# Mamba scan kernel: the sums over the states of two slots issued together, and a skip addition moved by one slot

## Chip, cores and metric

The kernel runs on one core of a Trainium2 chip, in one launch. The metric is the device time of the launch in microseconds (us); lower is better.

## What is computed

The reference applies two layers to x, of shape (4, 512, 64, 64), in float32. The first is a group norm, then a Mamba block run on four groups of 128 channels, then a projection; the second is a group norm and a linear attention. Both add their input. This case concerns the recurrence inside the Mamba block and what follows it:

```python
def step(h, inp):
    dt_t, B_t, C_t, x_t = inp
    dA = jnp.exp(dt_t[:, :, None] * A)
    h = dA * h + (dt_t * x_t)[:, :, None] * B_t[:, None, :]
    y = jnp.einsum('bds,bs->bd', h, C_t)          # sum over the 16 states
    return (h, y)
...
y = ys.transpose(1, 0, 2) + xc * D_param
y = y * jax.nn.silu(z)
return jnp.einsum('bld,od->blo', y, out_proj_w)
...
ym = ym + skip_scale * chunks                     # the skip addition
```

There are 256 inner channels, 16 states, and 4096 positions for each of 4 images and 4 channel groups.

## The kernel before, in words

The outer loop has 128 steps: image b (4), time tile t of 512 positions (8), channel group c (4). A step has 16 slots. A slot s covers one half e of the 256 inner channels, one quarter q of the states (4 of 16), and, by `jj`, two of the four blocks of 32 channels: partition 32k+i of a tile holds state k of the four and channel i of a block. So slots s = 0 to 7 are e = 0 and 8 to 15 are e = 1, and an even slot has blocks 0 and 1, the odd one after it blocks 2 and 3, with the same states. The global slot number is g.

What a slot does, in the order in which `slot` (from L457) emits it:

- `keep(g - 1)` (L494), on POOL: a copy of the last column of h, 128x2.
- `b_row` (L428), on SP, in odd slots: the rows of B for a later pair of slots, broadcast by four DMAs from DRAM.
- `drive(g + 1)` (L453), on POOL: the product of `d_all` and `b_all`, 128x1024, into a buffer `bx` for the next slot. There are three `bx` buffers, so it writes the one that slot g - 2 used.
- two scans (L470), on DVE, 128x512 each, reading `bx` and `dA`, writing h; after each a `decay` (L445) on ACT, the exponential for a later scan, into one of two PSUM banks.
- the multiply (L478), on DVE: h times `c_all`, written back into the same `bx`.
- in odd slots `c_row` (L84, named `c_all`), on PE: the rows of C for the next pair of slots, spread over the partitions into the only `c_all` bank.
- the sums over the states, here called the fold (L84, named `y<-bx,fold`), on PE: for each of the slot's two blocks a matmul of `bx` with a 128x32 matrix of ones and zeros, which adds four states and writes 32 partitions of the bank `y`. Four quarters accumulate there. `bx` is free when both are done.
- `after()`: everything else, spread over the slots by a fixed list and by three queues of pieces.

`after()` and `in_scan()` put this into the slots: `with_d` (L499, reads `y`) in slots 0 and 8; `gate` (L502, POOL) in 1 and 9; `time_banks` (`pt`, PE) in 1; the softplus (ACT) and `out_proj` (`po`, two PE matmuls for the step before) in 2; `with_skip` (L511, DVE, reads `po`) and `to_rows` (L370, a POOL product, and two DMAs) in 3; the pieces of `inputs` (`pc`, `pz`) in 3 to 7; silu in 10; `mixers` (`pd`) from 11. After these, one piece at most of the queue `late` (norms of the next time tile, projection of the last one) and one of `rest` (attention of the image before) is emitted, as long as a credit in matmul units lasts. All orders on all engines are fixed when the program is built (`manual_schedule`); an engine's instructions run in that order.

In float32 each matmul instruction appears in the trace as two weight loads and two passes.

Of the kernel before, what the change touches and what calls it, by code (L numbers as in the profile page):

```python
# [24 lines left out]
def kernel(  # L25
# [26 lines left out]
    NC = C // P  # L52
# [6 lines left out]
    BLK = 32  # L59
    KS = P // BLK  # L60
    NQ = NST // KS
    NJ = P // BLK
# [12 lines left out]
    def work_bank(name):  # L75
        return ps_w.tile([P, T], F32, tag="w", name=name)
# [4 lines left out]
    def mm(out_, lhsT, rhs, **how):  # L81

        work["mm"] += (0.25 if rhs.dtype == BF16 else 1.0) * rhs.shape[-1] / T
        nc.tensor.matmul(out_, lhsT, rhs, **how)  # L84

    work = {"mm": 0.0}
# [27 lines left out]
    for i in range(3):  # L114
        r = slice(i * LANE, (i + 1) * LANE)
# [6 lines left out]
    fold = const.tile([P, BLK], F32, tag="fold", name="fold")  # L122
    for k in range(KS):
        r = slice(k * BLK, (k + 1) * BLK)
# [83 lines left out]
    for o in range(NC):  # L208
        pw = work_bank(f"pw_{o}")
        for c in range(NC):  # L210
            mm(
                pw[:, 0:1], w_pr[:, c, o * P : (o + 1) * P], b_sb[:, c : c + 1],
                start=(c == 0), stop=(c == NC - 1),
# [45 lines left out]
    def bc(v, n):  # L259
        return v.unsqueeze(1).to_broadcast([P, n, v.shape[-1]])  # L260
# [152 lines left out]
    JJ = NJ // 2  # L413
    SLOTS = NH * NQ * JJ

    def place(g):

        n, r = divmod(g, SLOTS)
        e, r = divmod(r, NQ * JJ)
        return n, e, *divmod(r, JJ)  # L420

    b_all, c_all, dAs, bxs, hs, ys = {}, {}, {}, {}, {}, {}

    def b_row(g):
        n, e, q, _ = place(g)
        got = wk.tile([P, T], F32, tag="b_all", name=f"b_all_{g}", bufs=3)
        for k in range(KS):
            nc.sync.dma_start(  # L428
                got[k * BLK : (k + 1) * BLK, :],
                fs[n]["b_rows"][q * KS + k, :].partition_broadcast(BLK),  # L430
            )
        b_all[g // JJ] = got
# [16 lines left out]
    def drive(g):  # L449
# [5 lines left out]
        )  # L455

    def slot(g, last, in_scan, after):  # L457
        n, e, q, jj = place(g)
        b, t, c = steps[n]
        js = slice(jj * 2, jj * 2 + 2)  # L460
        if g:
            keep(g - 1)
        if g % JJ and g + 5 < last:
            b_row(g + 5)
        if g + 1 < last:
            drive(g + 1)
        h = hs[g] = wk.tile([P, 2, T], F32, tag="h", name=f"h_{g}", bufs=2)
        for i in range(2):
            j = jj * 2 + i
            nc.vector.tensor_tensor_scan(  # L470
                h[:, i, :], dAs.pop(2 * g + i), bxs[g][:, i, :],
                0.0 if t == 0 else st[b][:, c, e, q, j : j + 1], ALU.mult, ALU.add,
            )
            if 2 * g + i + LEAD < 2 * last:
                decay(2 * g + i + LEAD)
        in_scan()

        nc.vector.tensor_tensor(bxs[g], h, bc(c_all[g // JJ], 2), ALU.mult)  # L478
        if g % JJ and g + 1 < last:
            c_row(g + 1)  # L480
        if q == 0 and jj == 0:
            ys[n, e] = ps_y.tile([P, T], F32, tag="y", name=f"y_{n}_{e}")
        for i in range(2):
            r = slice((jj * 2 + i) * BLK, (jj * 2 + i + 1) * BLK)
            mm(ys[n, e][r, :], fold, bxs[g][:, i, :], start=(q == 0), stop=(q == NQ - 1))
        work["mm"] -= 1
        del bxs[g]
        after()

    def keep(g):  # L490

        n, e, q, jj = place(g)
        b, _, c = steps[n]
        nc.gpsimd.tensor_copy(st[b][:, c, e, q, jj * 2 : jj * 2 + 2], hs.pop(g)[:, :, T - 1])  # L494
# [9 lines left out]
    def out_proj(f, nm):  # L504
        f["po"] = work_bank(f"po_{nm}")
        for e in range(NH):
            mm(f["po"], w_op[:, e, :], f["xz"][:, 1, e, :], start=(e == 0), stop=(e == NH - 1))

    def with_skip(f, xn, c):
        v = xn[:, c, NTAP - 1 : NTAP - 1 + T]  # L510
        nc.vector.scalar_tensor_tensor(v, v, sk, f["po"], ALU.mult, ALU.add)  # L511
# [129 lines left out]
    steps = [(b, t, c) for b in range(B) for t in range(NT) for c in range(NC)]  # L641
# [3 lines left out]
    xn, pads = {}, {}  # L645
# [19 lines left out]
    def leave(b, t):  # L665
        if t == 0:
            stats1[b] = stats_tile(f"st1_{b}")
            x1s[b] = [
                dram.tile([P, NC, T], F32, tag="x1", name=f"x1_{b}_{i}", bufs=3 * NT)
                for i in range(NT)  # L670
            ]
        ym = xn[b, t][:, :, NTAP - 1 : NTAP - 1 + T]
        yield from projected(ym, stats1[b], x1s[b][t], b, t)
        if t == NT - 1:
            yield
            norms[b, 1] = stats_end(stats1[b], f"b{b}")
            rest.append(attention(b, x1s[b], norms[b, 1]))
            yield
# [8 lines left out]
    late, rest, light = [], [], []  # L687
# [30 lines left out]
    with tc.manual_schedule():  # L718
        credit = 0.0
        for n, (b, t, c) in enumerate(steps):  # L720
            f, nm = fs[n], names[n]
            before = fs[n - 1] if n else None
            nxt = fs[n + 1] if n + 1 < N else None
            front = step_inputs(n + 2) if n + 2 < N else iter(())
            mix = mixers(fs[n + 2], names[n + 2]) if n + 2 < N else iter(())
            if c == 0 and (t + 1 < NT or b + 1 < B):
                late.append(tile_norm(b, t + 1) if t + 1 < NT else tile_norm(b + 1, 0))
            if c == 0 and t == 0 and b + 1 < B:
                light.append(input_norm(b + 1))
                st[b + 1] = wk.tile([P, NC, NH, NQ, NJ], F32, tag="st", name=f"st_{b + 1}")  # L730
            if c == 2:
                while late and (b, t + 1) in xn and late[0].__name__ == "tile_norm":
                    one(late)
            for s in range(SLOTS):
                def in_scan():
                    if s == 0 and before is not None:
                        with_d(before, n - 1, 1)
                    if s == SLOTS // 2:
                        with_d(f, n, 0)

                def after():
                    nonlocal credit
                    start = work["mm"]
                    if s == 1:
                        spread(f, 1, nm)
                        if before is not None:
                            gate(before, 1)
                        if nxt is not None:
                            time_banks(nxt, names[n + 1])
                    if s == 2:  # L750
                        if nxt is not None:
                            nc.scalar.preload_act_table_set("softplus")
                            time_steps(nxt, names[n + 1])
                            nc.scalar.preload_act_table_set("natural_log_exp_and_others")
                        if before is not None:
                            out_proj(before, names[n - 1])
                    if s == 3:
                        if before is not None:
                            pb_, pt_, pc_ = steps[n - 1]
                            with_skip(before, xn[pb_, pt_], pc_)  # L760
                            if pc_ == NC - 1:
                                late.append(leave(pb_, pt_))
                        if nxt is not None:
                            to_rows(nxt, 0, names[n + 1])
                            to_rows(nxt, 1, names[n + 1])
                    if 3 <= s < 8:
                        next(front, None)
                    if s == 10 and n + 2 < N:
                        silu(n + 2)
                        nc.scalar.preload_act_table_set("natural_log_exp_and_others")  # L770
                    if s == 9:
                        gate(f, 0)
                        if nxt is not None:
                            spread(nxt, 0, names[n + 1])
                    if s >= 11:
                        next(mix, None)
                    if s in (2, 10):
                        one(light)
                        credit = 0.0
                        return  # L780
                    credit = min(credit + 3.2 - (work["mm"] - start), 3.2)
                    for queue in (late, rest):
                        if credit > 0:
                            start = work["mm"]
                            one(queue)
                            credit -= work["mm"] - start

                slot(n * SLOTS + s, N * SLOTS, in_scan, after)
            fs[n - 1].clear() if n else None
        keep(N * SLOTS - 1)  # L790
# [60 lines left out]
```

## Time and profile before

| what | value |
|---|---|
| median of 3 runs | 9795.15 us (9785.57 to 9796.92) |
| the profiled execution, its own time | 9786.31 us |
| its span in the profile | 9784.6 us |
| slots (steps), from the first scan to the last multiply | 123 us to 9299 us |
| DVE busy | 8325.7 us (85%) |
| PE busy, all matmuls | 7861.1 us (80%) |
| of which the fold, 8192 records | 2566.8 us |
| POOL busy | 6088.6 us (62%) |
| ACT busy | 5018.9 us (51%) |
| mean granted TensorE clock | 0.863 |

The profile's page gives the busy time of each engine, then the span in 40 slices, then groups of instructions with their busy time, the mean duration of one, and the idle time of the engine just before them with what ended it. The trace behind it can be asked for waits (who waited for whom) and for a timeline. The stretch after 9299 us has no slots: there the attention of the last image runs, with PE busy and DVE nearly idle.

### The profile page before, as it was taken

The numbers are of one execution on the slowest core, as the hardware profiler recorded it, in microseconds if no ns is written. First come the engines' busy times: TensorE is split into PE (matmuls) and PEld (weight loads), VectorE is DVE, ScalarE is ACT, GpSimd is POOL, SyncE is SP. The second block draws the span as 40 slices with busy tenths as digits, with TensorE's granted clock in tenths as the row PEclk, the third lists the DMA queues.
The fourth block names the chain that finished last, engine by engine and source line by source line (L and its number), as shares of the span: only waits on it lengthen the run. The fifth ranks groups of instructions, "written<-read, shape, count | busy, mean of one in ns | idle before, by whom it ended". The sixth has DMA issues, their size and how long they took to land.

```text
span 9784.6 us, 75975 instructions
## 1 busy us (share of the span) xinstructions
PE 7861.1 (80%) x20192; PEld 2424.5 (25%) x20192; DVE 8325.7 (85%) x7474; ACT 5018.9 (51%) x6944; POOL 6088.6 (62%) x4949
## 2 busy tenths in 40 slices
PE   5777777777788888888888888888888888888889
PEld 1111111111222222222222222222222222222244
DVE  6998898889899999888898989988988999988910
ACT  4554555555555555545555555555555555554421
POOL 3766666666666666666666666666666666666600
PEclk8777777777888889889888989989888989988999
DMA  5455444444545445545555554445554444555512
GB/s 145 122 125 126 108 113 116 117 116 120 134 121 132 120 117 128 124 124 146 137 131 129 125 128 116 117 120 137 151 127 117 123 120 121 122 124 134 143 37 78
DMA packets 628210, 1196.87 MB, mean 122 GB/s; under 512 B 116056, under 2 KB 116576, under 8 KB 615488
## 3 DMA queue, kind: packets, MB, share of 16 engines
q1 hardware_dynamic: 620928, 1187.44, 48.6%
q10 hardware_dynamic: 6848, 4.57, 0.2%
q8 instruction: 159, 2.61, 0.1%
q14 instruction: 275, 2.25, 0.1%
HBM read 986.04 MB, written 205.52 MB: 122 GB/s over the span
## 4 chain that ended last, share of the span: by engine, by line
PE 42%; DVE 38%; issue 11%; ACT 5%; DMA 3%; POOL 1%; SPq 0%; DVEq 0%; ACTq 0%; POOLq 0%
DVE h L470 27%; PE y L84 10%; PE pc L84 9%; DVE bx L478 7%; PE pq L84 4%; PE pt L84 3%; PE pr L84 3%; PE pp L84 3%; PE po L84 2%; PE c_all L84 2%; PE pd L84 2%; PE mu_b L84 2%; PE pz L84 1%; DVE xn L286 1%; ACT dA L445 1%
## 5 line engine op out<-in xcount | busy, mean ns | idle before, releaser
L453 POOL TENSOR_TENSOR bx<-d_all,b_all 128x1024 f32<-128x1024 f32 x2048 | 4824.3, 2356 | 251.4 <-PE y L84 170.7
L445 ACT ACTIVATE dA<-d_all,a_t 128x512 f32<-128x512 f32 x4096 | 2789.8, 689 | 3377.1 <-DVE h L470 3358.3
L470 DVE TENSOR_TENSOR_SCAN h<-dA,st,bx 128x512 f32<-128x512 f32 x3584 | 4391.8, 1267 | 140.4 <-ACT dA L445 138.8
L84 PE MATMUL y<-bx,fold 128*32 128x512 f32 x8192 | 2566.8, 709 | 630.0 <-DVE bx L478 628.3
L478 DVE TENSOR_TENSOR bx<-h,c_all 128x1024 f32<-128x1024 f32 x2048 | 2499.5, 1220 | 152.6 <-PE c_all L84 36.7
L494 POOL COPY st<-h 128x2 f32<-128x2 f32 x2048 | 380.1, 186 | 2639.9 <-DVE h L470 2498.7
L84 PE MATMUL c_all<-parts,sel 96*128 96x512 bf16 x1024 | 447.9, 437 | 1141.0 <-DVE bx L478 1140.9
L84 PE MATMUL pq<-w_qk,xa 128*128 128x512 f32 x2048 | 995.5, 614 | 1.5 <-ACT xa L252 1.5
L84 PE MATMUL pc<-xn,w_cv 128*128 128x512 f32 x2048 | 954.8, 609 | 4.6 <-ACT xn L290 4.6
L84 PEld LDWEIGHTS y<-bx,fold 128*32 128x32 f32 x8192 | 321.5, 115 | 2345.8 <-issue 1399.6
L470 DVE TENSOR_TENSOR_SCAN h<-dA,bx 128x512 f32<-128x512 f32 x512 | 596.4, 1206 | 35.4 <-ACT dA L445 17.6
L84 PE MATMUL pp<-xn,w_pr 128*128 128x512 f32 x1024 | 548.2, 662 | 4.2 <-DVE xn L286 4.2
L84 PE MATMUL pr<-xb,m 128*128 128x512 f32 x1024 | 512.9, 635 | 42.0 <-DMA xb<-x 42.0
L84 PEld LDWEIGHTS <-sel 96*128 96x128 bf16 x1280 | 127.2, 99 | 1631.2 <-DVE bx L478 1273.0
L84 PEld LDWEIGHTS pc<-xn,w_cv 128*128 128x128 f32 x2048 | 369.8, 190 | 595.2 <-issue 485.0
L84 PEld LDWEIGHTS pq<-w_qk,xa 128*128 128x128 f32 x2048 | 393.7, 197 | 474.6 <-issue 459.1
L343 ACT ACTIVATE xz<-pc,cb 128x512 f32<-128x512 f32 x256 | 175.9, 687 | 430.2 <-PE pc L84 430.2
L370 POOL TENSOR_TENSOR dt<-dt,xz 128x1024 f32<-128x1024 f32 x128 | 301.4, 2355 | 149.9 <-ACT dt L363 149.8
L561 DVE TENSOR_TENSOR kq<-pk,kq 128x512 f32<-128x512 f32 x124 | 85.3, 688 | 320.6 <-PE pk L84 320.6
L84 PE MATMUL pd<-xz,w_xp 128*120 128x512 f32 x512 | 356.1, 832 | 0.0
L84 PE MATMUL pt<-dtr,w_dt 8*128 8x512 f32 x512 | 351.7, 819 | 1.5 <-ACT dtr L395 1.5
L511 DVE SCALAR_TENSOR_TENSOR xn<-xn,sk,po 128x512 f32<-128x512 f32 x128 | 95.6, 747 | 298.5 <-PE po L84 298.5
(132 smaller groups left out, 6454.6 us busy)
## 6 DMA issues: line engine op xcount, KB each, us to landing
d_all<-d_rows SPq DMA_DIRECT2D x2048, 256.0 KB, 6.9
b_all<-b_rows SPq DMA_DIRECT2D x4096, 64.0 KB, 2.2
d_rows<-dt SPq DMA_DIRECT2D x256, 512.0 KB, 3.1
xs<-in_x_dram SPq DMA_DIRECT2D x32, 1024.0 KB, 11.9
xn<-in_x_dram SPq DMA_DIRECT2D x32, 1024.0 KB, 5.3
xr<-in_x_dram SPq DMA_DIRECT2D x32, 1024.0 KB, 5.3
x<-xr SPq DMA_DIRECT2D x32, 1024.0 KB, 4.3
xa<-x SPq DMA_DIRECT2D x32, 1024.0 KB, 5.5
```

The lines of the kernel that those rows point to most:

```text
L84: nc.tensor.matmul(out_, lhsT, rhs, **how)
L286: nc.vector.tensor_tensor(v, v, bc(var, NC), ALU.mult)
L343: nc.scalar.activation(xz[:, 0, e, :], pc[e], AF.Identity, bias=cb[:, e : e + 1])
L370: nc.gpsimd.tensor_tensor(f["both"][:, 1], f["both"][:, 0], f["xz"][:, 0], ALU.mult)
L445: nc.scalar.activation(dAs[k], fs[n]["d_all", e][:, 0, j, :], AF.Exp, scale=a_t[:, e, j, q : q + 1])
L453: nc.gpsimd.tensor_tensor(bxs[g], fs[n]["d_all", e][:, 1, jj * 2 : jj * 2 + 2, :], bc(b_all[g // JJ], 2), ALU.mult)
L470: nc.vector.tensor_tensor_scan(h[:, i, :], dAs.pop(2 * g + i), bxs[g][:, i, :], 0.0 if t == 0 else st[b][:, c, e, q, j : j + 1], ALU.mult, ...
L478: nc.vector.tensor_tensor(bxs[g], h, bc(c_all[g // JJ], 2), ALU.mult)
L494: nc.gpsimd.tensor_copy(st[b][:, c, e, q, jj * 2 : jj * 2 + 2], hs.pop(g)[:, :, T - 1])
L511: nc.vector.scalar_tensor_tensor(v, v, sk, f["po"], ALU.mult, ALU.add)
L561: nc.vector.tensor_tensor(kq, pk, kq, ALU.add)
```

## The change

The fold moves out of `slot` into a function of its own, which is called in odd slots only and does the four blocks of both slots of a pair one after the other: an even slot issues no matmul for `y`. Both `bx` buffers of the pair are let go there. The bookkeeping of matmul units for the credit comes to the same sum. In the loop, `with_skip` and, at the last channel group, the start of `leave` (which appends the projection's pieces to `late`) move from slot 3 to slot 4.

```diff
         nc.vector.tensor_tensor(bxs[g], h, bc(c_all[g // JJ], 2), ALU.mult)
         if g % JJ and g + 1 < last:
             c_row(g + 1)
-        if q == 0 and jj == 0:
+        if jj == JJ - 1:
+            fold_states(g)
+        after()
+
+    def fold_states(g):
+
+        n, e, q, _ = place(g)
+        if q == 0:
             ys[n, e] = ps_y.tile([P, T], F32, tag="y", name=f"y_{n}_{e}")
-        for i in range(2):
-            r = slice((jj * 2 + i) * BLK, (jj * 2 + i + 1) * BLK)
-            mm(ys[n, e][r, :], fold, bxs[g][:, i, :], start=(q == 0), stop=(q == NQ - 1))
-        work["mm"] -= 1
-        del bxs[g]
-        after()
+        for j in range(NJ):
+            mm(
+                ys[n, e][j * BLK : (j + 1) * BLK, :], fold, bxs[g + 1 - JJ + j // 2][:, j % 2, :],
+                start=(q == 0), stop=(q == NQ - 1),
+            )
+        work["mm"] -= 2
+        for i in range(JJ):
+            del bxs[g - i]
...
+                    if s == 4 and before is not None:
+                        pb_, pt_, pc_ = steps[n - 1]
+                        with_skip(before, xn[pb_, pt_], pc_)
+                        if pc_ == NC - 1:
+                            late.append(leave(pb_, pt_))
                     if s == 3:
-                        if before is not None:
-                            pb_, pt_, pc_ = steps[n - 1]
-                            with_skip(before, xn[pb_, pt_], pc_)
-                            if pc_ == NC - 1:
-                                late.append(leave(pb_, pt_))
                         if nxt is not None:
                             to_rows(nxt, 0, names[n + 1])
                             to_rows(nxt, 1, names[n + 1])
```

## The prediction, as recorded before the changed kernel ran

> **What bounds the kernel now.** I read the busy times and the groups first. After each group stand its busy time, the mean duration of one, and the idle time just before it.
>
> ```profile
> PE 7861.1 (80%) x20192; PEld 2424.5 (25%) x20192; DVE 8325.7 (85%) x7474; ACT 5018.9 (51%) x6944; POOL 6088.6 (62%) x4949
> ...
> PEclk8777777777888889889888989989888989988999
> ...
> L453 POOL TENSOR_TENSOR bx<-d_all,b_all 128x1024 f32<-128x1024 f32 x2048 | 4824.3, 2356 | 251.4 <-PE y L84 170.7
> ...
> L470 DVE TENSOR_TENSOR_SCAN h<-dA,st,bx 128x512 f32<-128x512 f32 x3584 | 4391.8, 1267 | 140.4 <-ACT dA L445 138.8
> L84 PE MATMUL y<-bx,fold 128*32 128x512 f32 x8192 | 2566.8, 709 | 630.0 <-DVE bx L478 628.3
> L478 DVE TENSOR_TENSOR bx<-h,c_all 128x1024 f32<-128x1024 f32 x2048 | 2499.5, 1220 | 152.6 <-PE c_all L84 36.7
> ```
>
> DVE sets the pace: up to 9304 us, where the slots end, it sits idle only about 900 us. Then the waits on DVE in that stretch (us in total, times, longest):
>
> ```profile
> DVE xn L511 <- PE po L84: 298.5, 88, 6.7
> DVE h L470 <- ACT dA L445: 156.4, 145, 3.4
> DVE xr L324 <- PE pp L84: 79.9, 57, 2.4
> ...
> DVE kq L561 <- PE pk L84: 58.2, 42, 3.0
> DVE xn L270 <- PE mu_b L84: 52.3, 31, 2.0
> DVE bx L478 <- PE c_all L84: 36.7, 22, 3.7
> ```
>
> A third of the idle time is the skip addition waiting for `po` in slot 3; most of the rest also waits for PE. Then the timeline, PE first, POOL second, DVE third, at one odd slot:
>
> ```profile
> 5009.02 0.38 PE L84 MATMUL c_all<-parts,sel 96*128 96x512 bf16 x1
> 5009.33 1.05 PE L84 MATMUL y<-bx,fold 128*32 128x512 f32 x4
> 5010.31 1.13 PE L84 MATMUL pz<-xn,w_z 128*128 128x512 f32 x2
> ```
>
> ```profile
> 5006.58 2.35 POOL L453 TENSOR_TENSOR bx<-d_all,b_all 128x1024 f32<-128x1024 f32 x1
> 5010.07 0.18 POOL L494 COPY st<-h 128x2 f32<-128x2 f32 x1 [1.14 <-DVE h L470]
> 5010.48 2.36 POOL L453 TENSOR_TENSOR bx<-d_all,b_all 128x1024 f32<-128x1024 f32 x1 [0.23 <-PE y L84]
> ```
>
> ```profile
> 5002.79 1.22 DVE L478 TENSOR_TENSOR bx<-h,c_all 128x1024 f32<-128x1024 f32 x1
> 5003.93 2.45 DVE L470 TENSOR_TENSOR_SCAN h<-dA,st,bx 128x512 f32<-128x512 f32 x2
> 5006.41 1.22 DVE L478 TENSOR_TENSOR bx<-h,c_all 128x1024 f32<-128x1024 f32 x1
> ```
>
> A bare slot takes DVE 3.62 us (5006.41 - 5002.79). The fold occupies PE 0.98 us (5009.33 to 5010.31), and a drive follows a fold's start by 1.15 us.
>
> **What the Trainium skill says.** "TensorEngine Tiling (Array Packing)", section Tiling Modes: 128 rows by 32 columns gives four tiles that run independently. The trace agrees for two: a fold's four records start 0, 7, 453 and 460 ns after the first, so both tiles run each pass side by side. Four are not in it. "TensorE: Matmul & The Clock Gate", Part 3: three column tiles measured 2.38x. That speaks for four going together; no run here shows it. The same page, Part 1: PE's clock halves after a quiet window of about 3.4 us. The trace agrees: the clock is at half for 2687.6 us, in stretches that are multiples of 3.4 us, and then a fold's second pass starts 855 instead of 453 ns after the first.
>
> **The fold, on PE.** The same 8192 passes, but in 1024 groups of four tiles. If four go as two do, a group costs 0.98 + 2 x 0.007, say 1.0 us, and the 1024 groups of even slots go: about 1000 us of PE at full clock. From below the gain could be nothing (two pairs in turn, 1.96 us). I take four together. PE isn't the bound; this pays only through waits.
>
> **The fold, on POOL: a new wait.** The drive of slot o+2 (o odd) reuses the buffer of the even slot before o. Today that is free a slot earlier; then it comes free only with the group after o's multiply. Queued behind that drive on POOL are the copy L494 and the next drive; the scan of o+2 waits for it. From the end of o's multiply to that scan:
> - full clock: 0.36 (`c_all` first, least delay seen in odd slots) + 1.15 + 2.36 + 0.04 (POOL to DVE) = 3.91 us;
> - half clock: 0.59 + 2.01 + 2.36 + 0.04 = 5.00 us, with the delays of the half-clock folds.
>
> A bare pair gives 3.54 to 3.61 us. So I took from the trace, for every odd slot, the DVE work and the idle time between its multiply's end and the scan two slots on. Two choices are mine. First, half of the present idle time there stays, since PE, which causes it, loses 1 us in about 6 per pair. Second, the half-clock share: now 0.41, 0, 0.10, 0.28, 0.66, 0.22, 0.34 for slots 1, 5, 7, ... 15. It rises, as PE's idle time gathers just ahead of each group. For this there is an indication: the first 512 slots, without attention work, show 0.44 of their folds at half clock, the others 0.16. Means per window in us; the two floors are means of the greater of (work + half the idle) and 3.91 or 5.00:
>
> | slot | work + idle | floor 3.91 | floor 5.00 | share | x128, us |
> |---|---|---|---|---|---|
> | 1 | 4.17 + 0.59 | 4.63 | 5.28 | 0.55 | +29 |
> | 5 | 4.60 + 1.13 | 5.21 | 5.63 | 0.10 | -61 |
> | 7 | 5.08 + 0.24 | 5.20 | 5.63 | 0.30 | +1 |
> | 9 | 4.01 + 0.21 | 4.32 | 5.14 | 0.60 | +77 |
> | 11 | 4.38 + 1.25 | 5.04 | 5.53 | 0.70 | -32 |
> | 13 | 4.83 + 0.28 | 4.98 | 5.45 | 0.50 | +13 |
> | 15 | 4.47 + 0.27 | 4.61 | 5.20 | 0.55 | +24 |
>
> For slot 9: 0.4 x 4.32 + 0.6 x 5.14 - 4.22 = 0.60, x 128 = 77. Sum: +51.
>
> **The skip addition, slot 3 to 4.** Its own 747 ns stay in the window of slot 3 (4.31 work + 2.35 idle), so only the wait counts. But `po` is late because PE is behind, and PE runs `c_all` and the group of slot 3 behind `po`. In place of the skip, the scan of slot 5 waits until 3.9 us after `po`. `po` itself comes earlier: slot 2's fold, which stood ahead of it, is gone, 0.98 us at full and 1.9 at half clock; with almost half of slot 2's folds at half clock, 1.4 us. So in each window of slot 3 I took 1.4 off the wait, and then the greater of the window's work, 3.91, and the rest of the wait + 3.9: a mean of 5.50 instead of 6.66, x 128 = -148 us, not -298. With 0.7 us earlier it is 5.90 (-97), with 1.9 it is 5.25 (-180).
>
> **Backlog.** Slots 3 and 4 issue 6.84 us of other matmuls (16 passes of 0.428), with the group 8.2 against 8.1 us of DVE work, so slot 5 inherits lateness: 0.2 us x 128 = 25. Half-clock stretches elsewhere: I add 30 more, from 0 to 110 together. Total +55.
>
> **Costed at nothing.** `leave` one slot later: `tile_norm`'s dozen pieces stand ahead of it in `late`; without them one piece in each of 32 tiles would shift, 1 us each at most. `b_row`'s DMA on SP waits for a drive some 2 us longer, and what is queued there behind it with it; its rows are used four slots (14 us) later and land in 2.2. On POOL `to_rows` (2.36) in slot 3 now ends about when the group does; at most another 0.2 us per step, 25 us, within the backlog's range. No DMA or POOL work is added.
>
> **Sum.** -148 + 51 + 55 = -42 on 9786 for the profiled execution: 9744. The median of the runs shown (9795) is 9 above that execution: about 9750.
>
> **Rivals.**
> 1. *The new wait wins (slower).* PE goes quiet between groups and sits at half clock: shares 0.70, 0.15, 0.40, 0.75, 0.80, 0.65, 0.70, three quarters of the idle stays, `po` comes only 0.7 earlier. The same table gives +222, then -97 + 80: +205, or 10000. With half of the idle staying, it decides once more than about 0.62 of the groups outside slots 3 and 5 start at half clock (mean of the shares now 0.33, in the forecast 0.53). For it: a slower DVE makes PE quieter still. Against: at half clock the same work fills PE twice as long, which ends quiet windows.
> 2. *Relief wins.* Shares stay, a quarter of the idle remains, `po` 1.9 earlier, no backlog: -155 - 180 = -335, or 9460. For it: nearly every DVE wait names PE. Against: the quarter of the run with less PE work has the slower clock.
> 3. *Four tiles don't run together*: the groups take 0.98 (full) or 1.9 (half) more, floors 4.89 and 6.9. The table over all eight slots gives +836: 10630. Against: two do run together.
>
> **Chances.** Forecast 0.43 (own range 9660 to 9880), rival 1 0.35, rival 2 0.17, rival 3 0.05. A measurement of this kernel tells about 0.2% from no change (20 us). Faster: rival 2 and 0.7 of the forecast, 0.47; within 0.2%: 0.08; slower 0.45. The range 9440 to 10080 leaves out rival 3 (0.05), the upper quarter of rival 1 (0.09) and the lower third of rival 2 (0.06).
>
> **What would show it.** Right: `y` busy near 1100 to 1500 us with eight records per group starting within 30 ns per pass; the wait of the skip for `po` gone; new waits of DVE h (L470) on POOL bx (L453), and of POOL on PE y, some hundreds of times each, most at slots 1, 9 and 11. Wrong: few such waits (rival 2), a clock below 0.80 (rival 1), records of a group starting in two pairs (rival 3).

## The result, and the profile after

The changed kernel takes 9942.35 us (median of 4 runs, 9941.46 to 9956.8), the one before 9796.03 us (4 runs, 9785.57 to 9803.79). The ratio on record is 1.0154 (the medians alone give 1.0149), with a 95% interval of 1.0136 to 1.0171: slower by 1.5%, where 0.5% faster was forecast. The profiled execution took 9941.5 us, 155 more than that of before. From the first multiply to the last it is 153 us longer; the stretch ahead of that is 5 us longer, the one behind it 3 us shorter.

The page of the changed kernel, the lines that answer to those shown of before:

```profile
PE 7108.6 (72%) x20192; PEld 2467.3 (25%) x20192; DVE 8370.9 (84%) x7474; ACT 5014.6 (50%) x6944; POOL 6023.3 (61%) x4949
...
PEclk7677776677788888878878878878878888887899
...
L453 POOL TENSOR_TENSOR bx<-d_all,b_all 128x1024 f32<-128x1024 f32 x2048 | 4817.9, 2353 | 2786.7 <-PE y L84 2655.7
L470 DVE TENSOR_TENSOR_SCAN h<-dA,st,bx 128x512 f32<-128x512 f32 x3584 | 4395.4, 1268 | 484.3 <-POOL bx L453 396.7
...
L84 PE MATMUL y<-bx,fold 128*32 128x512 f32 x8192 | 1479.8, 803 | 1.7 <-DVE bx L478 1.7
```

The change does on PE what it says: the fold is busy for 1480 us instead of 2567, and PE as a whole for 752 us less (at the lower clock, 0.798 against 0.863, its other work takes 335 us more). But POOL's drive waits 2656 us for the fold, where it waited 171, and the scan waits for the drive. The waits on DVE, up to the end of the slots (us in total, times, longest); the first fence is one line of before, for the wait that grew:

```profile
DVE h L470 <- POOL bx L453: 18.6, 3, 15.8
```

```profile
DVE h L470 <- POOL bx L453: 484.9, 599, 16.2
DVE h L470 <- ACT dA L445: 89.2, 148, 4.5
...
DVE bx L478 <- PE c_all L84: 57.9, 50, 3.2
DVE kq L570 <- PE pk L84: 52.9, 28, 3.1
DVE xr L324 <- PE pp L84: 42.3, 43, 1.4
DVE xn L270 <- PE mu_b L84: 37.1, 30, 2.0
```

The wait of the skip addition for `po` (298.5 us) is gone, and 484.9 us of a wait that was 18.6 stand in its place. One group and what hangs on it, in the timeline of PE, of POOL and of DVE, with the clock at half for the first group and at full for the second:

```profile
5009.45 0.59 PE L84 MATMUL c_all<-parts,sel 96*128 96x512 bf16 x1 [3.45 <-DVE bx L478]
5009.97 1.94 PE L84 MATMUL y<-bx,fold 128*32 128x512 f32 x8
...
5018.09 0.38 PE L84 MATMUL c_all<-parts,sel 96*128 96x512 bf16 x1 [0.80 <-DVE bx L478]
5018.39 1.07 PE L84 MATMUL y<-bx,fold 128*32 128x512 f32 x8
5019.39 0.39 PE L84 MATMUL pq<-bqk,sel 96*128 96x512 bf16 x1
```

```profile
5011.99 2.35 POOL L453 TENSOR_TENSOR bx<-d_all,b_all 128x1024 f32<-128x1024 f32 x1 [3.66 <-PE y L84]
```

```profile
5008.18 1.22 DVE L478 TENSOR_TENSOR bx<-h,c_all 128x1024 f32<-128x1024 f32 x1
...
5012.34 1.22 DVE L478 TENSOR_TENSOR bx<-h,c_all 128x1024 f32<-128x1024 f32 x1
5014.37 2.34 DVE L470 TENSOR_TENSOR_SCAN h<-dA,bx 128x512 f32<-128x512 f32 x2 [0.81 <-POOL bx L453]
```

The multiply of the odd slot ends at 5009.40 (5008.18 + 1.22). `c_all` and eight fold records follow, two passes for each of four tiles; the drive starts at 5011.99, the scan at 5014.37: 4.97 us from multiply to scan, the 5.00 of the forecast's half-clock floor. At full clock the group of eight records occupies PE for 1.00 us (5018.39 to 5019.39), against 0.98 for four records before.

The added 153 us in the slots are 61 us of idle stretches over 0.15 us, 47 us of shorter ones, 42 us in which DVE's instructions overlap less, and 3 us by which they are longer in sum. A scan that waits for nothing starts 0.08 us before the multiply ahead of it ends (5003.93 against 5002.79 + 1.22 in the trace of before); the scan at 5014.37 starts after the drive that it waits for. So a wait costs more than the idle time that is booked for it: 599 waits of 0.08 us would be 48 us, an estimate.

By odd slot, the window of the forecast (from the multiply's end to the scan two slots on), means in us, from the two traces. "Bound" counts those of the 128 windows (127 for slot 15) in which the scan starts within 0.06 us of the drive's end; the share is that of the groups whose first record starts at half clock:

| slot | before | forecast | after | bound | half-clock share forecast, found |
|---|---|---|---|---|---|
| 1 | 4.76 | 4.99 | 5.21 | 91 | 0.55, 0.49 |
| 3 | 6.65 | 5.50 | 5.70 | 97 | 0.15, 0.16 |
| 5 | 5.73 | 5.25 | 5.51 | 58 | 0.10, 0.01 |
| 7 | 5.32 | 5.33 | 5.51 | 35 | 0.30, 0.20 |
| 9 | 4.22 | 4.81 | 4.89 | 110 | 0.60, 0.59 |
| 11 | 5.63 | 5.38 | 5.71 | 71 | 0.70, 0.77 |
| 13 | 5.11 | 5.22 | 5.36 | 76 | 0.50, 0.43 |
| 15 | 4.74 | 4.93 | 5.07 | 64 | 0.55, 0.46 |

### The profile page after: what moved, and what is told of

It is laid out like the page before. It is cut to its first block, busy times and chain, and to the rows that moved or that the text cites. A ratio compares the mean times of both kernels' runs of the same rounds, so it can differ in the third digit from the quotient of the medians.

```text
span 9939.8 us, 76399 instructions
## 1 busy us (share of the span) xinstructions
PE 7108.6 (72%) x20192; PEld 2467.3 (25%) x20192; DVE 8370.9 (84%) x7474; ACT 5014.6 (50%) x6944; POOL 6023.3 (61%) x4949
## 4 chain that ended last, share of the span: by engine, by line
PE 40%; DVE 30%; POOL 13%; issue 10%; DMA 5%; ACT 2%; SPq 1%; POOLq 0%; DVEq 0%; ACTq 0%
DVE h L470 20%; POOL bx L453 11%; PE y L84 9%; PE pc L84 8%; DVE bx L478 7%; PE pt L84 4%; PE pq L84 3%; PE po L84 3%; PE c_all L84 3%; DMA d_all<-d_rows 2%; PE pr L84 2%; PE pp L84 2%; PE pd L84 2%; PE mu_b L84 2%; DVE xn L286 1%
## 5 line engine op out<-in xcount | busy, mean ns | idle before, releaser
L84 PE MATMUL y<-bx,fold 128*32 128x512 f32 x8192 | 1479.8, 803 | 1.7 <-DVE bx L478 1.7
L84 PE MATMUL pq<-w_qk,xa 128*128 128x512 f32 x2048 | 1034.3, 642 | 1.9 <-ACT xa L252 1.9
L84 PE MATMUL pc<-xn,w_cv 128*128 128x512 f32 x2048 | 926.1, 605 | 4.6 <-ACT xn L290 4.6
L84 PEld LDWEIGHTS y<-bx,fold 128*32 128x32 f32 x8192 | 179.5, 121 | 2017.2 <-issue 2002.0
L84 PE MATMUL pr<-xb,m 128*128 128x512 f32 x1024 | 540.7, 675 | 46.6 <-DMA xb<-x 34.9
L84 PEld LDWEIGHTS pq<-w_qk,xa 128*128 128x128 f32 x2048 | 426.3, 210 | 507.3 <-issue 488.0
L84 PE MATMUL pt<-dtr,w_dt 8*128 8x512 f32 x512 | 414.1, 951 | 1.5 <-ACT dtr L395 1.5
L84 PE MATMUL pd<-xz,w_xp 128*120 128x512 f32 x512 | 399.6, 926 | 0.0
L84 PE MATMUL po<-xz,w_op 128*128 128x512 f32 x512 | 361.9, 847 | 17.8 <-ACT dt L363 16.7
L511 POOL TENSOR_TENSOR xz<-xz 128x512 f32<-128x512 f32 x256 | 325.0, 1270 | 3.1 <-DVE xz L508 3.1
```

Source lines behind the costliest of these rows:

```text
L511: nc.gpsimd.tensor_tensor(f["xz"][:, 1, e, :], f["xz"][:, 1, e, :], f["xz"][:, 0, e, :], ALU.mult)
```

## The experiments

My theory after the result: the late release of the even slot's buffer costs what was forecast, and the relief that was to pay for it is smaller. Rivals: the lower clock of PE (0.798 against 0.863) costs it; or the moved skip addition does harm.

**e1, the skip addition moved, nothing else.** The diff of the loop alone, on the kernel before.

> The kernel before with the skip addition (and the start of the projection) one slot later; the sums are issued per slot as before. Buffer-wait theory (what costs is the product's wait for the buffer that the late sums hold; the moved skip is a gain): most of the 298.5 us wait for po goes, part of it comes back as later waits, 9550 to 9650 us. Backlog theory (PE is behind in slots 2 to 5 whatever DVE waits for, so the wait only changes its name): 9730 to 9800 us.

Measured 9789.9 us, ratio 0.9996 (0.9987 to 1.0004): no difference. The wait for `po` is gone, and these have taken its place (over the whole run they were 156.4, 36.7 and 55.0 us):

```profile
DVE h L470 <- ACT dA L445: 292.1, 303, 2.4
...
DVE bx L478 <- PE c_all L84: 163.0, 138, 4.3
...
DVE xn L270 <- PE mu_b L84: 81.3, 32, 2.7
```

The window of slot 3 fell from 6.65 to 5.54 us, that of slot 5 rose from 5.73 to 6.64. My own expectation fell; the measured time is that of the backlog theory. But it isn't PE alone that is behind. DVE meets PE's lateness one instruction further on at `c_all`. The waits for dA are of three kinds. 117 us of them, in both kernels, are those of slot 12's scan, and in the 5 us before it ACT is busy without a gap with silu of slot 10 and the table loads (1.28 us each) on both sides of it: this is ACT's own work. From the groups of before:

```profile
L685 ACT ACTIVATE xz<-xz 128x2048 f32<-128x2048 f32 x128 | 244.5, 1910 | 1.4
...
L685 ACT ACT_TABLE_LOAD x127 | 162.9, 1283 | 2.2
```

100 us are new (2 us before), at slot 4's scan: there the exponentials stand on ACT behind the softplus of slot 2, with two table loads too, which had itself waited for `pt`, 0.5 us on average. And at slots 6 and 7, where the exponentials stand behind ACT's wait for `pc` (430 us before, 726 now), 27 us have become 65.

**e2, the grouped sums alone**: the changed kernel with the skip addition back in slot 3.

> The changed kernel with the skip addition put back into slot 3: the grouped sums alone. Buffer-wait theory: slower than the changed kernel, but by less than 298 us, since po comes earlier and the wait for po and the wait for the buffer lie in the same window: 9970 to 10080 us. If the moved skip did nothing or harm: 9940 us or less.

Measured 9957.2 us, ratio 1.0166 (1.0151 to 1.0182), between the two expectations. It is 15 us above the changed kernel, but the intervals of the two ratios overlap, so what the moved skip is worth beside the grouping isn't shown. The grouping makes the loss.

**e4, four `bx` buffers.**

```diff
-        bxs[g] = wk.tile([P, 2, T], F32, tag="bx", name=f"bx_{g}", bufs=3)
+        bxs[g] = wk.tile([P, 2, T], F32, tag="bx", name=f"bx_{g}", bufs=4)
...
-    w_qk = const_rows(wqk, "w_qk")
+    w_qk = const_rows(wqk[:, 0:C], "w_qk")
...
-                            pq, gn[:, c, u * P : (u + 1) * P], w_qk[:, c, j * C : (j + 1) * C],
+                            pq, gn[:, c, u * P : (u + 1) * P], w_qk[:, c, :],
```

> The changed kernel with four bx buffers instead of three. To make room, the weights of the attention's q and k are only the first half, used for both, so that part of the result differs; the instructions and their shapes are the same. Buffer-wait theory: the waits of DVE h on POOL bx and of POOL bx on PE y nearly vanish, although the clock stays low: 9350 to 9600 us. Clock theory: 9850 us or more.

Measured 9649.0 us, ratio 0.9854 (0.9838 to 0.9871): 293 us faster than with three buffers, at the same low clock (0.803). No window is bound by POOL any more. It was to be below 9600; it isn't, since DVE still waits for dA and `c_all` (71.4 us), as in e1:

```profile
DVE h L470 <- ACT dA L445: 288.7, 294, 2.4
```

PE is busy for 809 us less than before, but it waits 2410 us for DVE's multiplies, where it waited 1769 (1141 ahead of `c_all`, 628 ahead of the fold): most of what was freed became PE's own waiting.

**e8, the control for it**: four buffers and the moved skip addition, sums per slot as before.

> Control for the run with four buffers: the kernel before with four bx buffers and the skip addition one slot later, with the same halved attention weights. If the fourth buffer matters only where the sums are grouped: 9740 to 9800 us, as with three. If four buffers help by themselves, by slack between POOL and DVE: 9650 us or less, and the price of the buffer wait read from the other run is too high.

Measured 9796.1 us, ratio 0.9999 (0.9991 to 1.0008). The fourth buffer does nothing by itself. So the buffer wait costs 293 us (9942 - 9649), and the grouping with the moved skip, freed of it, gains 146 us against before (1.46%).

**e3, the group ahead of `c_all`.**

```diff
-        if g % JJ and g + 1 < last:
-            c_row(g + 1)
         if jj == JJ - 1:
             fold_states(g)
+        if g % JJ and g + 1 < last:
+            c_row(g + 1)
```

> The changed kernel with the group of four sums ahead of c_all on PE instead of behind it. Buffer-wait theory: c_all (0.31 us at full clock, 0.5 at half) leaves the chain from multiply to scan in some 600 bound windows, 204 x 0.31 + 398 x 0.5 = 262 us at most; 9700 to 9820 us. Clock theory (PE is slower, and that delays all that DVE needs of it): no change, 9900 to 9960 us.

Measured 9605.0 us, ratio 0.9807 (0.9792 to 0.9821): the fastest that computes the whole reference, 337 us below the changed kernel, more than the 262 that `c_all` could free. The trace shows why. With `c_all` behind the group, the first instruction of the group waits for the even slot's multiply alone; with `c_all` ahead of it, it can't start before the odd multiply is done, since `c_all` waits for that. PE's timeline in e3:

```profile
5016.33 1.05 PE L84 MATMUL y<-bx,fold 128*32 128x512 f32 x4
5019.02 1.05 PE L84 MATMUL y<-bx,fold 128*32 128x512 f32 x4 [1.63 <-DVE bx L478]
5020.00 0.39 PE L84 MATMUL c_all<-parts,sel 96*128 96x512 bf16 x1
5020.32 3.54 PE L84 MATMUL pt<-dtr,w_dt 8*128 8x512 f32 x4
5023.80 3.77 PE L84 MATMUL pp<-xn,w_pr 128*128 128x512 f32 x4
5027.37 1.91 PE L84 MATMUL po<-xz,w_op 128*128 128x512 f32 x4
5029.21 1.07 PE L84 MATMUL y<-bx,fold 128*32 128x512 f32 x8
5030.21 0.39 PE L84 MATMUL c_all<-parts,sel 96*128 96x512 bf16 x1
5030.44 7.03 PE L84 MATMUL pc<-xn,w_cv 128*128 128x512 f32 x16
5037.40 1.06 PE L84 MATMUL y<-bx,fold 128*32 128x512 f32 x8
```

Where PE is early (5016), the even slot's two tiles go on their own and let their buffer go; only the other two wait for the odd multiply. Where PE is late (5029 and 5037, slots 3 and 5, after 9 us of `pt`, `pp` and `po` without a gap), both multiplies are done, and all four tiles run together in 1.0 us. In 270 of 1024 groups all four start within 0.1 us of each other, 210 of them in slots 3 and 5; in the changed kernel in all but the last.

**e5, the same order, but with the odd slot's tiles first**, so that the group can't come apart.

```diff
-        for j in range(NJ):
+        for j in (2, 3, 0, 1):
```

> As the run with the sums ahead of c_all, but inside the group the two tiles of the odd slot come first, so that all four wait for the odd slot's multiply and stay one group (y busy near 1450 us, not 2245). Chain theory (that run gained because c_all left the chain): about the same gain, 9620 to 9750 us. Early-release theory (it gained because the even slot's two tiles no longer wait for the odd slot's multiply, and let their buffer go early): most of the gain is lost, 9780 to 9900 us.

Measured 9773.5 us, ratio 0.9977 (0.9969 to 0.9986), between the two ranges. All 1024 groups stay whole, and 506 windows are bound. So of e3's 337 us, `c_all` out of the chain is 169 (9942 - 9774), and the early release with all that it brings is the other 169.

**e9, the group split around `c_all`**: even tiles, `c_all`, odd tiles.

```diff
-        if g % JJ and g + 1 < last:
-            c_row(g + 1)
         if jj == JJ - 1:
-            fold_states(g)
+            fold_states(g, range(2))
+            if g + 1 < last:
+                c_row(g + 1)
+            fold_states(g, range(2, NJ))
```

> The changed kernel with the group split: the even slot's two tiles first, then c_all, then the odd slot's two tiles (skip addition in slot 4). Early-release theory (what the grouping costs is the even slot's buffer held until behind the odd multiply and c_all; what it gains is that PE no longer stands still for the even multiply): as fast as the run with the sums ahead of c_all or faster, since c_all is early again and DVE's 178 us of waits for it go: 9430 to 9600 us. If that run's gain lay in c_all being last: 9650 us or more.

Measured 9850.9 us, ratio 1.0067 (1.0052 to 1.0082). I had expected the fastest kernel; the time lies in the range that I had given to the other theory, that e3's gain lay in `c_all` being last. But the buffer's way isn't longer than in e3 (157 bound windows against 161), and the early release is there: slots 1, 9 and 15 have windows of 4.65, 4.26 and 4.76 us, near those before. But with `c_all` between them the four tiles never run together (none of 1024 groups), the fold is busy for 2552 us again, and the window of slot 5 is 6.85 us, against 5.44 in e3: 180 of the 246 us between the two. Where PE is late, running four together is worth something after all; e3 has that and the early release.

**e12, the same with the skip addition in slot 3.**

> As the split run, with the skip addition back in slot 3. If the moved skip is worth something only once PE is not behind: slower than the split run by 60 to 200 us. If PE in slots 2 to 5 bounds both the same way, as in the first run: within 20 us of it.

Measured 9839.4 us, ratio 1.0056 (1.0039 to 1.0073): as in e1, the place of the skip addition makes no difference that can be measured.

**e10, e3 with four buffers** (and the attention weights of e4).

> The run with the sums ahead of c_all, with four bx buffers besides (and the halved attention weights). Only the 161 bound windows left in it, 67 us of waits, can go: 9530 to 9600 us. If the fourth buffer takes 150 us or more, the buffer still bound that run by more than its waits show.

Measured 9550.7 us, ratio 0.9757 (0.9742 to 0.9772), 54 us below e3, as its few bound windows (161) let expect.

**e6, the kernel before with the moved skip and, in odd slots, the sums ahead of `c_all`.**

> The kernel before (sums per slot), with the skip addition one slot later, and in odd slots the sums ahead of c_all. If the gain of the sums ahead of c_all is that of the shorter way to the buffer, and the place of the even slot's sums doesn't matter: 9560 to 9650 us. If it needs the even slot's sums behind that slot's other matmuls (so that PE doesn't stand still for the even multiply): 9720 to 9800 us.

Measured 9776.1 us, ratio 0.9981 (0.9972 to 0.9991). It differs from e3 only in the even slot's sums, which stand ahead of that slot's other matmuls: they make PE stop for the even multiply, and can't run with the odd slot's. The two together are worth 171 us.

**e7 and e11, the clock.** One unused matmul of constants, in every even slot (e7), or only in slots 0, 8, 10, 12 and 14 (e11):

```diff
         after()
+        if jj == 0:
+            nc.tensor.matmul(work_bank(f"warm_{g}"), ones_c, w_pr[:, 0, :], start=True, stop=True)
```

> The changed kernel with one more matmul in each even slot, behind the other work, of constants into a work bank that nobody reads: about the PE time that the grouping saved (0.86 us at full clock), put where PE is idle. Clock theory (half clock after quiet stretches makes the bound windows long): the granted clock rises to 0.85 or more and the time falls by 60 to 150 us, to 9790 to 9880. Buffer-wait theory without the clock: 9930 to 10030 us.

> The changed kernel with the unused matmul only in slots 0, 8, 10, 12 and 14, where PE has room, and not in slots 2, 4 and 6. From the run with it in every even slot, the windows of slots 1, 9, 11, 13 and 15 were 0.53 us per step shorter than in the changed kernel, 68 us in all, and those of 3 and 5 longer. If that is the price of the half clock: 9860 to 9890 us. If it is noise of the schedule: 9930 us or more.

e7: 10058.1 us, ratio 1.0269 (1.0254 to 1.0285). The clock rose to 0.852, and the windows of slots 1, 9, 11, 13 and 15 became 0.53 us per step shorter, but those of slots 3 and 5 became 1.5 us longer, where PE is behind and the extra matmul is only load. e11: 9899.0 us, ratio 1.0118 (1.0103 to 1.0133), clock 0.84: 43 us faster than the changed kernel, between my two expectations. The half clock is real, and by these two runs it is a small part of the loss: some 40 to 70 us of the 293. Neither brings the clock back to 0.863, and the extra matmul is load too, so it may be worth somewhat more.

**e13 to e16, PE's backlog.** The five pieces of the input projections moved from slots 3 to 7 into slots 5 to 9, in the kernel before, in that of e1, in the changed one and in e3.

```diff
-                    if 3 <= s < 8:
+                    if 5 <= s < 10:
```

> The kernel before with the five pieces of the input projections (pc, pz) in slots 5 to 9 instead of 3 to 7. Backlog theory (PE is behind in slots 2 to 6): somewhat faster, by less than the wait for po (which stands ahead of these pieces and stays): 9720 to 9790 us. If PE's load there doesn't matter: 9780 to 9830 us.

> The same with the skip addition in slot 4. Backlog theory: now that PE is less behind in slots 3 and 4, the moved skip is worth something: at least 60 us faster than with it in slot 3, 9600 to 9710 us. If the wait for po overlapped with something else: within 20 us of the run with it in slot 3.

> The changed kernel with the input projections in slots 5 to 9. The buffer wait stays (500 or more bound windows); backlog theory: 9820 to 9910 us; otherwise 9930 us or more.

> The run with the sums ahead of c_all, with the input projections in slots 5 to 9. Backlog theory: 9450 to 9570 us, the fastest of all that compute everything. If the four sums that run together when PE is late already made up for the backlog: 9590 to 9620 us.

Measured: e13 10096.3 us (ratio 1.0312, 1.0298 to 1.0326), e14 9986.6 (1.0200, 1.0186 to 1.0214), e15 10035.3 (1.0251, 1.0237 to 1.0265), e16 9726.8 (0.9935, 0.9921 to 0.9948). All four are slower than their counterparts, by 93 to 304 us, which I had not expected. DVE's waits in e14:

```profile
DVE xz L499 <- PE y L84: 317.2, 167, 4.8
DVE h L470 <- ACT dA L445: 277.0, 264, 3.4
```

The load has only gone on to slots 5 to 7, just ahead of `with_d` in slot 8, which reads `y` and had waited 34.3 us for it in e1. But the pair e13 and e14 answers what it was made for: with the input pieces out of slots 3 and 4, the same move of the skip addition gains 110 us, where it gained nothing that can be measured in e1. The windows show it: in e1 slot 3 loses 1.11 us and slot 5 gains 0.91; here slot 3 loses 0.82 us and slot 5 gains 0.10.

## Why the prediction was wrong, point by point

- *Four tiles run together at 1.0 us a group*: right (1.00 us; fourth tile 20 ns after the first). About 1000 us of PE gone at full clock: the fold's busy time fell by 1087 us, PE's by 752.
- *A new wait of POOL on the buffer, with floors of 3.91 and 5.00 us*: right in place and kind, most at slots 9, 3 and 1 (the forecast had named 1, 9 and 11). The 421 bound windows whose `c_all` starts within 0.1 us of the multiply's end average 4.01 us at full and 4.96 at half clock: the floors. In the other 181 PE is still busy when the multiply ends, and they average 5.64. The price as forecast is the table's +51 and the half of the idle that it takes off, 1.99 us per step (half the sum of the idle column) x 128 = 254: 305 us together. Measured, by the fourth buffer: 293. That the two are so near is luck in part: of the 293, 232 lie in the seven windows of the table.
- *The half-clock share rises as PE goes quiet ahead of the groups*: right, within 0.10 in all eight slots.
- *"half of the present idle time there stays"*: this is the step that failed. In e4, where no buffer wait hides it, the idle time of the table's seven windows is 3.88 us per step, of 3.96 before: 98% stays, where I took 50% (90% without slot 5, which takes over lateness from slot 3). Redone with the shares that were found, the forecast's table gives +28 us with half of the idle and +250 with all of it; measured are +224. The reason that I gave, PE "causes it" and loses 1 us in about 6, was wrong twice. For 117 us of these 507 (3.96 x 128) DVE waits for dA while ACT is at its own silu (e1), and a shorter fold does nothing for that. And where PE is the cause it is late behind other work, while the time that it gained fell where it waits for DVE anyway (e4: 641 us more of that). "Nearly every DVE wait names PE" speaks for relief only where PE has time left at that place.
- *The skip addition, -148*: the window of slot 3 is 122 us shorter in all, and 134 in e4, so the term was a little too large; but it isn't the moved addition alone that does this, for in e2, with the addition in slot 3, that window is 63 us shorter too. That the lateness comes back one pair later I had priced at 25 us in slot 5; it is 31 in e4 and 116 in e1, without the grouping.
- *Backlog, +55*: what the added 153 us have outside these eight windows is 51 us. That is luck: it is made of lost overlap and short waits, of which the forecast says nothing.
- *Together*: +224, -122 and +51 against +51, -148 and +55. Of the 195 us by which the slots missed the forecast, 173 lie in the windows where the idle time stayed.
- *Costed at nothing*: nothing in the runs speaks against that.
- *The rivals*: the first, the new wait wins, is what came, with its sign, a clock below 0.80, just met (0.797 to 0.800). Its 10000 us is 58 too high. Its +222 for the seven windows is what was measured, but by luck: it had shares of 0.65 to 0.80 in five of seven slots, which were 0.43 to 0.77, and let a quarter of the idle go, which stayed. With the shares found and three quarters of the idle, the table gives +138. The other two rivals didn't come: 599 such waits, and four tiles that start together.

Not settled: how the 169 us between e3 and e5 divide between the early release and PE's not standing still. The two can't be parted while the same instruction does both. Nor was it tried whether e4, with four buffers, would have had more relief at the clock of before: its clock is 0.803.

## What to carry to other kernels

Before batching work of one engine to save its time, look for the buffer that the batch holds longer: the way from the last producer through the batch and the refill to the next use (here 3.9 to 5.0 us) has to fit into the pitch of the bound engine where that has nothing else to do (3.6), not on average. A wait of the bound engine on another is worth removing only where that other engine isn't late; otherwise it comes back under other names (298 us of waits gone, nothing gained). A wait that names an engine says nothing of which work keeps that engine late; look there before pricing what less work of another kind will bring. The order in a queue can give both ends: with what can wait put behind the batch, the batch comes apart when there is time and packs itself when there is none (e3: 1.9% faster than before).

## What the runs showed of the hardware that I had not expected

Four column tiles that stand next to each other in PE's queue with waits of their own run together when the waits are already met: in e3, 270 groups start all four tiles within 0.1 us, the others in two pairs. The records show the first passes of all tiles together, and the second ones 453 ns later (855 at half clock). With one matmul in between that uses all 128 columns (`c_all` in e9) none of the 1024 groups does.

The clock doesn't ask for a quiet PE to go to half. The two main traces, cut into windows of 3.413 us from the clock's own changes, show in the slots: at full clock, all 528 windows in which PE's records (their ends are modelled) fill less than 0.4 are followed by half clock, and 54 of 2784 with more than 0.5; only 65 of the 528 are nearly quiet (under 0.05). At half clock, 1 of 924 windows filled to less than 0.8 is followed by full clock, and 679 of 938 filled to more than 0.9. The forecast had spoken of a quiet window.
